# ScalarE pieces of their own and an earlier self-attention in the plan of a decoder layer

## The chip, the cores and the metric

The kernel runs on one core of a Trainium2 chip. It is one program that holds its data in SBUF and PSUM and gives work to TensorE (PE; matmuls and transposes), VectorE (DVE), ScalarE (ACT), GpSimd (POOL) and, for the DMA queues, SyncE (SP). The metric is the device time of one execution in microseconds. A time is a median of several runs; the profile is one execution of its own.

## What is computed

The reference is one decoder layer over x of 16 batches, 512 rows and 256 columns, in fp32. Cut to what matters:

```
# 1 self-attention without softmax, two key/value sets, 16 heads
q  = x + x Wq + bq;  k_i = x + x Wk_i + bk_i;  v_i = x + x Wv_i + bv_i      (i = 0, 1)
state = prod_i ( (k_i / 32)^T (v_i / 32) )            # per batch and head
x1 = layernorm( x + layernorm_gb(q state) Wo + bo )
# 2 cross-attention on 64 context rows per batch, 16 heads of 64
x2 = layernorm( x1 + softmax(q k^T / 8, masked) v Wout + b_out )
# 3 eight experts: softmax routing; each expert takes at most 1024 rows, in order
x3 = layernorm( x2 + sum_e w_e * relu(x2 W1_e) W2_e )    # rows past the capacity get no expert
```

With these inputs the capacity of 1024 rows is used up by the first two batches (the "head"), so the other 14 batches end with the last layer norm, and the loop over further batches at the end of the program runs zero times.

## The kernel before, in words

**Tiles.** A batch is four tiles of 128 rows. Self-attention (L614 to L726) never forms k and v: the stream of Gram matrices computes x^T x (ps_g, L555 and L560, and one transposed block ps_gt, L573) and key sums (ps_ks, L585); from them a batch takes ps_gk (L629), the two states (ps_s, L641), transposes of x (ps_t, L233), ps_m and ps_b from the state, then four pieces ps_o (L687), each followed on VectorE by an addition and the layer norm's statistics (L249, L250). `normalized` (L252 to L269) is the layer norm: on ScalarE a logarithm and an exponential of the variance (L261, L262), on VectorE the offset (`off`, L265), on ScalarE one Identity for each of four tiles (L267). Transposes of the result (ps_zt, L700), four pieces ps_p (L711), the second norm into x1 and the transposes to x1T follow; at the end POOL adds a bias to x1 (L725). Before the second norm a batch waits in the plan until routing of the batch two before is done, since x1 has two buffers. xt, z, zT and pT have one buffer each.

**Cross-attention** (L765 to L843). The keys are multiplied into the query weights once per two batches (kq, ps_kq, L751), the values into the output weights during set-up (ps_vo, L492): their product goes through four buffers `vst` (copies by ScalarE L186 or VectorE L188), is stored in 128 DMAs of 132 KB (L497) to vo_dram, and is fetched again as `vo` (L781, 512 DMAs, eight chunks a batch, of which six are fetched ahead). For each tile there are two halves: ps_sim (L814), on VectorE the maximum (L820) and the subtraction (L821), on ScalarE the exponential (L822). Then the softmax: sum and reciprocal on VectorE (L800, L801), the multiply on POOL (L802), and a transpose on VectorE into pT (L804). When all four tiles are in pT, ps_x follows (L834): 256 matmuls of 32 rows in a row, and an addition (L841).

**Routing** (L846 to L873) is a layer norm, for the head a transpose to head_T, and a softmax over eight experts in small VectorE operations (L858 to L865) with one exponential (L861). `ranks` (L875 to L920) gives each row its place in its expert, once. The **experts** (L929 to L976) are ps_h (L946), a Relu copy to hT on VectorE or ScalarE in turn (L954, L952), ps_e (L963) and a weighted addition (L970).

**The order of the work.** It is fixed when the program is built. Each stage is a Python generator in a `Stream`; `weave` (L1010 to L1027) takes one piece after the other, up to the next `yield`, from the ready stream with the smallest planned time `at + span * spent / total`. `spent` grows by `model.took`, TensorE's time for the piece as the planner's class `Model` (L28 to L102) reckons it. After `yield WAIT` a stream is ready only when its own work would be done, by the same reckoning; `until(...)` yields until a condition holds; `beside(st, gen)` adds a small stream that starts at the present time of `st`. `in_order` (L1029) then pins the instructions of PE, DVE, ACT and POOL in the order in which they were traced; each engine works in that order and stops at an instruction whose input is not ready. SP's DMAs are issued in their traced order too. With SETUP = 115 and STEP = 78, self-attention of batch b is planned at SETUP + (b − 1) · STEP (L1071), cross-attention at SETUP + b · STEP, routing at SETUP + (b + 1) · STEP, the experts from SETUP + 1.3 · STEP on.

Of the kernel before, what the change touches and what calls it, by code (L numbers as in the profile page):

```python
# [27 lines left out]
class Model:  # L28
# [2 lines left out]
    WIDE = {"PE": 0.25, "DVE": 0.15, "Activation": 0.15, "Pool": 0.15}  # L31

    def __init__(self, nc):
        self.nc, self.free, self.dma = nc, {}, 0.0
        self.made, self.used, self.slots, self.rows, self.seen = {}, {}, {}, P, 0

    def tile(self, name, key, bufs):
# [28 lines left out]
    def run(self):  # L66

        traced = self.nc.cur_bb.bb.instructions
        end = now = self.free.get("PE", 0.0)
        self.took = 0.0  # L70
        for ins in traced[self.seen:]:
            kind, engine = type(ins).__name__, str(ins.engine).split(".")[-1]
            aps = [[a.bass_ap for a in l if hasattr(a, "bass_ap")] for l in (ins.ins, ins.outs)]
            names = [[a.name for a in l] for l in aps]
            at = 0.0
            for made, used, l in ((1, 0, names[0]), (1, 1, names[1])):
                for n in l:
                    if kind == "InstDMACopy" and self.made.get(n, (0, 0))[1] == "SP":
                        continue
                    for known, book in ((made, self.made), (used, self.used)):  # L80
                        if known and n in book:
                            t, by = book[n]
                            at = max(at, t + (self.WIDE.get(by, 0.0) if by != engine else 0.0))
            if kind == "InstDMACopy":
                size = 4 * min(a.size() for l in aps for a in l)
                start = max(at, self.dma if now < 40 else 0.0)
                self.dma = start + size / 220e3
                done = self.dma + 2.0
            elif names[1]:
                start = max(at, self.free.get(engine, 0.0))  # L90
                done = self.free[engine] = start + self.duration(ins, kind, engine)
                if engine == "PE":
                    self.took += done - start
                else:
                    end = max(end, done + 0.15)
            else:
                continue
            for n in names[0] + names[1]:
                self.used[n] = max(self.used.get(n, (0.0, None)), (done, engine), key=lambda p: p[0])
            for n in names[1]:  # L100
                self.made[n] = (done, engine)
        self.seen, self.end = len(traced), end  # L102
        return end
# [13 lines left out]
def decoder_layer(  # L117
# [134 lines left out]
    def normalized(dst, src, NT=NT, mm=None):  # L252


        rstd = small.tile([P, NT], FP, tag="rstd", name="rstd")
        if mm is None:
            mm = moments(NT)
            for t in range(NT):
                moment(mm, t, src(t))
        mv = mm[1]  # L260
        nc.scalar.activation(rstd, mv[:, :, 1], AF.Ln, bias=eps)  # L261
        nc.scalar.activation(rstd, rstd, AF.Exp, scale=-0.5)  # L262
        yield WAIT
        off = small.tile([P, NT], FP, tag="off", name="off")
        nc.vector.scalar_tensor_tensor(off, mv[:, :, 0], -1.0, rstd, ALU.mult, ALU.mult)  # L265
        for t in range(NT):
            nc.scalar.activation(  # L267
                dst[:, t, :], src(t), AF.Identity, bias=off[:, t:t + 1], scale=rstd[:, t:t + 1]
            )  # L269


    with ExitStack() as att:
# [492 lines left out]
        def cross_attention(b, x1, x1T):  # L765


            bl = b % GB
            if bl == 0:
                yield from context_group(b // GB)  # L770
            kq = group[b // GB][:, :, bl].rearrange("p c r h j -> p c (r h j)")


            vos = []

            def load_vo():
                c = len(vos)
                t = wk2.tile([P, NH // 4, CX], FP, tag="vo", name="vo", bufs=6)
                h0 = c % 4 * NH // 4
                for q in range(P // 32):  # L780
                    nc.sync.dma_start(  # L781
                        out=t[q * 32:(q + 1) * 32], in_=vo_dram[b, c // 4 * 32:(c // 4 + 1) * 32, h0:h0 + NH // 4, :]
                    )
                vos.append(t)

            def load_first():
                yield from until(lambda: ("values", b // (B // 2)) in held)
                for _ in range(6):
                    load_vo()

            beside(cross_st, load_first())

            probsT = wk1.tile([P, 2 * NH, NT, 32], FP, tag="pT", name="pT")
            ready = []

            def softmax(t, s):
                sm = small.tile([P, NH], FP, tag="sm", name="sm")
                nc.vector.tensor_reduce(sm, s, AX.X, ALU.add)  # L800
                nc.vector.reciprocal(sm, sm)  # L801
                nc.gpsimd.tensor_mul(s, s, sm.unsqueeze(2).to_broadcast([P, NH, J]))  # L802
                yield WAIT
                nc.vector.transpose(probsT[:, :, t, :], s.rearrange("p h (a j) -> p (h a) j", a=2))  # L804
                ready.append(t)

            for t in range(NT):
                yield from until(lambda: len(ready) > t - 2)
                s = wk2.tile([P, NH, J], FP, tag="s", name="s")
                mx = small.tile([P, NH], FP, tag="mx", name="mx")  # L810
                for hf in range(2):
                    ps = bank("ps_sim")
                    for cc in range(NC):
                        nc.tensor.matmul(  # L814
                            ps, x1T[:, cc, t * P:(t + 1) * P], kq[:, cc, hf * 512:(hf + 1) * 512],
                            start=(cc == 0), stop=(cc == NC - 1),
                        )
                    hs = slice(hf * 8, (hf + 1) * 8)
                    sim = ps.rearrange("p (h j) -> p h j", j=J)
                    nc.vector.tensor_reduce(mx[:, hs], sim, AX.X, ALU.max)  # L820
                    nc.vector.tensor_sub(s[:, hs, :], sim, mx[:, hs].unsqueeze(2).to_broadcast([P, 8, J]))  # L821
                    nc.scalar.activation(s[:, hs, :], s[:, hs, :], AF.Exp, scale=SCALE)  # L822
                    yield
                beside(cross_st, softmax(t, s))
            yield from until(lambda: len(ready) == NT)
            yield from until(lambda: made(probsT))
            yield from until(lambda: len(vos) == 6 and made(*vos))
            ps = [bank("ps_x") for _ in range(NT)]
            for c in range(8):
                for i in range(NH // 4):  # L830
                    blk = (c % 4 * NH // 4 + i) * 2 + c // 4
                    for q in range(NT):
                        pq = slice(q * 32, (q + 1) * 32)
                        nc.tensor.matmul(  # L834
                            ps[q][:, :CX], probsT[pq, blk].rearrange("p t i -> p (t i)"), vos[c][pq, i, :],
                            start=(c == 0 and i == 0), stop=(c == 7 and i == NH // 4 - 1),
                        )
                if c < 2:
                    load_vo()
            for q in range(NT):  # L840
                nc.vector.tensor_add(x1[:, q, :], ps[q][:, :CX], x1[:, q, :])  # L841
            yield WAIT
# [167 lines left out]
        def weave():  # L1010
            model.run()
            while streams:
                clock = model.free["PE"] = model.free.get("PE", 0.0)
                now = [st for st in streams if st.ready <= clock]
                if not now:
                    model.free["PE"] = min(st.ready for st in streams)
                    continue
                st = min(now, key=Stream.time)
                wait = next(st.gen, "end")
                st.end = max(st.end, model.run())  # L1020
                st.spent += model.took
                if wait == "end":
                    streams.remove(st)
                elif wait == WAIT:
                    st.ready = st.end
                else:
                    st.ready = clock + (wait or 0.0)  # L1027
# [40 lines left out]

        def all_self_attention():
            for b in range(B):  # L1070
                self_st.plan(SETUP + (b - 1) * STEP, STEP, 16.5)  # L1071
                yield from until(lambda: b in grams and sums[b // QB][1] and "rb" in cs and made(grams[b], sums[b // QB][1][0]))
                yield from self_attention(b, done)

# [137 lines left out]
```

## Time and profile before

| | us |
|---|---|
| median of three runs | 1387.47 (1385.21 to 1389.51) |
| the profiled execution | 1389.4 |
| its span in the profile | 1387.6 |
| TensorE busy | 1365.9 |
| VectorE busy | 850.7 |
| ScalarE busy | 402.2 |
| GpSimd busy | 203.7 |

The mean clock granted to TensorE in the profiled execution was 0.994 of full speed. The chain of work that ended last runs for 89% of the span through TensorE, 5% through VectorE and 2% through DMA. By groups, the largest are ps_h (L946) with 239.1 us, ps_sim (L814) with 235.0 and ps_x (L834) with 234.9 us. DMA moved 153.57 MB, 111 GB/s in the mean.

How to read it: "busy" is the time that records of an engine cover; TensorE's records are pipelined, so a busy TensorE is not always one at its full pace. In a row of a group or a timeline, `out<-in` are the program's names of the tiles; in brackets is the idle time before an instruction and who ended it. A row of waits names the waiting instruction, the one that released it, the sum in us, the count and the longest. PEclk is the granted clock, in tenths in the slices and as a share in the tables by stage.

### The profile page before, as it was taken

What the parts mean: (1) busy time and instruction counts of PE and PEld (TensorE: products, weight loads), DVE (VectorE), ACT (ScalarE), POOL (GpSimd) and SP (SyncE); (2) the same over time, 40 slices, a digit from 0 to 9 for tenths busy, and PEclk for the clock granted to TensorE, in tenths of its full rate; (3) what the DMA queues carried; (4) which work ended last, traced back from release to release, by engine and by line L of the source; (5) the groups of instructions that cost most, each with busy time, mean ns of one, the idle gap of its engine ahead of it and who ended that gap; (6) DMA issues with size and microseconds to landing.
All of it is one profiled execution on the core that took longest, in us unless ns stands there. A gap on an engine that the chain in (4) does not pass through costs nothing.

```text
span 1387.6 us, 24209 instructions
## 1 busy us (share of the span) xinstructions
PE 1365.9 (98%) x9630; PEld 1077.9 (78%) x9630; DVE 850.7 (61%) x1957; ACT 402.2 (29%) x912; POOL 203.7 (15%) x140
## 2 busy tenths in 40 slices
PE   8999999999999999999999999999999999999997
PEld 5766576877878787878878787878888787878686
DVE  2445848466584848475584848475665939484744
ACT  1134224132232314142233323142323323232322
POOL 0001112112020111112020112112020202111200
PEclk9999999999999999999999999999999999999999
DMA  8657775511515153522606053513334061505211
GB/s 260 203 136 191 189 195 163 142 32 42 145 53 150 46 142 106 127 77 52 181 24 164 31 142 106 126 62 77 110 95 123 16 187 46 147 26 126 91 56 40
DMA packets 98372, 153.57 MB, mean 111 GB/s; under 512 B 15560, under 2 KB 70096, under 8 KB 98256
## 3 DMA queue, kind: packets, MB, share of 16 engines
q1 hardware_dynamic: 98256, 151.98, 40.1%
q8 instruction: 78, 1.28, 0.4%
q14 instruction: 38, 0.31, 0.1%
HBM read 114.71 MB, written 37.22 MB: 109 GB/s over the span
## 4 chain that ended last, share of the span: by engine, by line
PE 89%; DVE 5%; DMA 2%; SPq 1%; ACT 1%; issue 1%; ACTq 0%; DVEq 0%
PE ps_x L834 16%; PE ps_sim L814 15%; PE ps_e L963 15%; PE ps_h L946 15%; PE ps_gk L629 4%; PE ps_p L711 4%; PE ps_o L687 3%; PE ps_kv L437 3%; PE ps_t L233 2%; PE ps_kq L751 2%; PE ps_vo L492 2%; PE ps_s L641 2%; PE ps_g L555 2%; PE ps_zt L700 1%; PE ps_m L670 1%; PE ps_g L560 1%
## 5 line engine op out<-in xcount | busy, mean ns | idle before, releaser
L946 PE MATMUL ps_h<-head_T,wi 128*128 128x256 f32 x1024 | 239.1, 379 | 0.0
L834 PE MATMUL ps_x<-vo,pT 32*128 32x264 f32 x4096 | 234.9, 384 | 3.9 <-DVE pT L804 3.7
L814 PE MATMUL ps_sim<-kq,x1T 128*128 128x512 f32 x512 | 235.0, 593 | 0.0
L834 PEld LDWEIGHTS ps_x<-vo,pT 32*128 32x128 f32 x4096 | 211.5, 186 | 26.1 <-issue 5.6
L946 PEld LDWEIGHTS ps_h<-head_T,wi 128*128 128x128 f32 x1024 | 193.4, 190 | 38.8 <-issue 13.0
L802 POOL TENSOR_TENSOR s<-s,sm 128x1024 f32<-128x1024 f32 x64 | 121.7, 1901 | 539.8 <-DVE sm L801 501.4
L841 DVE TENSOR_TENSOR x<-ps_x,x 128x264 f32<-128x264 f32 x64 | 23.2, 426 | 226.3 <-PE ps_x L834 226.3
L822 ACT ACTIVATE s<-s 128x512 f32<-128x512 f32 x128 | 80.7, 630 | 276.1 <-DVE s L821 276.0
L814 PEld LDWEIGHTS ps_sim<-kq,x1T 128*128 128x128 f32 x512 | 94.5, 190 | 83.2 <-issue 74.5
L820 DVE TENSOR_REDUCE mx<-ps_sim 128x8 f32<-128x512 f32 x128 | 86.1, 673 | 42.0 <-PE ps_sim L814 41.6
L821 DVE TENSOR_TENSOR s<-ps_sim,mx 128x512 f32<-128x512 f32 x128 | 88.5, 692 | 4.4
L725 POOL TENSOR_TENSOR x<-x,bout 128x1056 f32<-128x1056 f32 x16 | 38.7, 2420 | 320.7 <-ACT hT L952 172.6
L804 DVE STREAM_TRANSPOSE pT<-s 128x1024 f32<-128x1024 f32 x64 | 78.6, 1228 | 7.0 <-POOL s L802 7.0
L952 ACT ACTIVATE hT<-ps_h 128x256 f32<-128x256 f32 x128 | 46.9, 376 | 119.9 <-PE ps_h L946 119.8
L701 ACT ACTIVATE zT<-ps_zt,shift,gain 128x512 f32<-128x512 f32 x32 | 23.2, 775 | 189.5 <-PE ps_zt L700 189.5
L800 DVE TENSOR_REDUCE sm<-s 128x16 f32<-128x1024 f32 x64 | 77.1, 1204 | 0.4 <-ACT s L822 0.4
L261 ACT ACTIVATE rstd<-bn_mv,eps 128x4 f32<-128x4 f32 (+1 forms) x70 | 20.7, 295 | 159.5 <-DVE bn_mv L250 156.0
L267 ACT ACTIVATE x<-x,off,rstd 128x264 f32<-128x264 f32 (+1 forms) x112 | 58.3, 591 | 29.3 <-DVE off L265 29.3
L687 PE MATMUL ps_o<-m,xT 128*128 128x264 f32 x256 | 66.7, 387 | 0.0
L954 DVE TENSOR_SCALAR hT<-ps_h 128x256 f32<-128x256 f32 x128 | 52.2, 409 | 22.5 <-PE ps_h L946 22.3
L711 PE MATMUL ps_p<-wo,zT 128*128 128x264 f32 x256 | 63.1, 387 | 0.0
L629 PE MATMUL ps_gk<-wk,g 128*128 128x256 f32 x256 | 61.2, 382 | 0.0
(174 smaller groups left out, 1897.4 us busy)
## 6 DMA issues: line engine op xcount, KB each, us to landing
vo<-vo_dram SPq DMA_DIRECT2D x512, 132.0 KB, 4.2
vo_dram<-vst SPq DMA_DIRECT2D x128, 132.0 KB, 2.4
xt<-in_x_dram SPq DMA_DIRECT2D x16, 512.0 KB, 4.0
wi<-L_ffn_experts_inter_dram SPq DMA_DIRECT2D x8, 1024.0 KB, 5.3
gx<-in_x_dram SPq DMA_DIRECT2D x15, 512.0 KB, 4.2
x_rest<-x SPq DMA_DIRECT2D x14, 512.0 KB, 3.1
out_dram<-x SPq DMA_DIRECT2D x14, 512.0 KB, 2.9
kT<-k_dram SPq DMA_DIRECT2D x8, 512.0 KB, 3.3
```

What stands on the lines that cost most here:

```text
L629: nc.tensor.matmul(ps[:, :C], blk, wk[:, j, k, :], start=(j == 0), stop=(j == NC - 1))
L687: nc.tensor.matmul(ps[:, :CX], xT[:, cc, t * P:(t + 1) * P], m[:, cc, :], start=(cc == 0), stop=(cc == NC - 1))
L711: nc.tensor.matmul(ps[:, :CX], zT[:, cc, t * P:(t + 1) * P], wo[:, cc, :], start=(cc == 0), stop=(cc == NC - 1))
L802: nc.gpsimd.tensor_mul(s, s, sm.unsqueeze(2).to_broadcast([P, NH, J]))
L804: nc.vector.transpose(probsT[:, :, t, :], s.rearrange("p h (a j) -> p (h a) j", a=2))
L814: nc.tensor.matmul(ps, x1T[:, cc, t * P:(t + 1) * P], kq[:, cc, hf * 512:(hf + 1) * 512], start=(cc == 0), stop=(cc == NC - 1),)
L820: nc.vector.tensor_reduce(mx[:, hs], sim, AX.X, ALU.max)
L821: nc.vector.tensor_sub(s[:, hs, :], sim, mx[:, hs].unsqueeze(2).to_broadcast([P, 8, J]))
L822: nc.scalar.activation(s[:, hs, :], s[:, hs, :], AF.Exp, scale=SCALE)
L834: nc.tensor.matmul(ps[q][:, :CX], probsT[pq, blk].rearrange("p t i -> p (t i)"), vos[c][pq, i, :], start=(c == 0 and i == 0), stop=(c == 7 ...
L946: nc.tensor.matmul(ps[:, :TB], wi[:, cc, f * P:(f + 1) * P], head_T[b][:, cc, t0 * P:t0 * P + TB], start=(cc == 0), stop=(cc == NC - 1),)
L963: nc.tensor.matmul(ps[:, :C], hT[f][:, t * P:(t + 1) * P], wo_[:, f, :], start=(f == 0), stop=(f == NF - 1),)
```

## The change

There are three edits, and the number of instructions on each engine stays the same.

1. `normalized` gets a `yield WAIT` ahead of the logarithm and one ahead of the four Identities, so that both ScalarE steps are pieces of their own.
2. In cross-attention the exponential of each half becomes a small stream of its own, put beside; the softmax of a tile waits in the plan until both of its halves are done. Since the planner now runs more than once within a piece, `took` is set to zero in `weave`.
3. Self-attention of batch b is planned at SETUP + (b − 1.6) · STEP in place of (b − 1).

```diff
@@ Model.run
         traced = self.nc.cur_bb.bb.instructions
         end = now = self.free.get("PE", 0.0)
-        self.took = 0.0
@@ normalized
         mv = mm[1]
+        yield WAIT
         nc.scalar.activation(rstd, mv[:, :, 1], AF.Ln, bias=eps)
         nc.scalar.activation(rstd, rstd, AF.Exp, scale=-0.5)
         yield WAIT
         off = small.tile([P, NT], FP, tag="off", name="off")
         nc.vector.scalar_tensor_tensor(off, mv[:, :, 0], -1.0, rstd, ALU.mult, ALU.mult)
+        yield WAIT
         for t in range(NT):
@@ cross_attention
-            def softmax(t, s):
+            def exponentials(s, hf, halves):
+                hs = slice(hf * 8, (hf + 1) * 8)
+                nc.scalar.activation(s[:, hs, :], s[:, hs, :], AF.Exp, scale=SCALE)
+                halves.append(hf)
+                yield
+
+            def softmax(t, s, halves):
+                yield from until(lambda: len(halves) == 2 and made(s))
                 sm = small.tile([P, NH], FP, tag="sm", name="sm")
...
+                halves = []
                 mx = small.tile([P, NH], FP, tag="mx", name="mx")
...
-                    nc.scalar.activation(s[:, hs, :], s[:, hs, :], AF.Exp, scale=SCALE)
+                    model.run()
+                    beside(cross_st, exponentials(s, hf, halves))
                     yield
-                beside(cross_st, softmax(t, s))
+                beside(cross_st, softmax(t, s, halves))
@@ weave
                 st = min(now, key=Stream.time)
+                model.took = 0.0
                 wait = next(st.gen, "end")
@@ all_self_attention
-                self_st.plan(SETUP + (b - 1) * STEP, STEP, 16.5)
+                self_st.plan(SETUP + (b - 1.6) * STEP, STEP, 16.5)
```

More of the change, by code (lines that the diff above doesn't have):

```diff
@@ L33, in __init__ @@
     def __init__(self, nc):
-        self.nc, self.free, self.dma = nc, {}, 0.0
+        self.nc, self.free, self.dma, self.took = nc, {}, 0.0, 0.0
         self.made, self.used, self.slots, self.rows, self.seen = {}, {}, {}, P, 0
```

## The prediction

> **What bounds the kernel now.** I read the page's busy shares and slices first, then TensorE's waits, then a table by stage, and last the timelines of the queues behind the waits that the table left.
>
> ```profile
> PE 1365.9 (98%) x9630; PEld 1077.9 (78%) x9630; DVE 850.7 (61%) x1957; ACT 402.2 (29%) x912; POOL 203.7 (15%) x140
> ...
> PE   8999999999999999999999999999999999999997
> ```
>
> TensorE is the bound, and no other engine is near. The change removes no matmul: both built programs have 5060 matmuls, 1957 VectorE, 912 ScalarE and 789 DMA instructions. Only order and waits can pay. How much is there to win? I took each matmul kind's pitch from stretches without a wait (the 256-column one 0.432 us: two records of 0.216; 512 columns 0.858; 264 columns 0.445; a batch's 256 ps_x records 14.15) and multiplied by the counts: 1334.8 us. With 3.1 us before the first matmul and 6.7 after the last one's start, 1387.6 − 1344.6 = 43 us are excess. By place: 7.7 in 0–50 us, 4.0 in 50–100, 12.9 in 100–200, 3.1 in 200–300, 5.1 in 300–350, then 0.05 to 0.6 for each 50 us, and 3.9 after 1250. So a change of order can win something between 50 and 340 us, and little else.
>
> ```profile
> PE ps_x L834 <- DVE pT L804: 3.7, 2, 3.2
> ...
> PE ps_e L963 <- DVE hT L954: 1.8, 1, 1.8
> PE ps_vo L492 <- DVE u L570: 0.8, 1, 0.8
> PE ps_vo L492 <- ACT st L186: 0.7, 1, 0.7
> ```
>
> The next table has microseconds, busy time of PE, PEld, DVE, ACT, POOL, then granted clock, DMA share and GB/s.
>
> ```profile
> 66.70:73.50 6.80, 6.80 (x26) 5.96 (x26) 2.18 (x3) 0.00 (x0) 0.00 (x0) 0.50 0.00 0
> 107.00:143.00 36.00, 35.38 (x213) 23.80 (x212) 19.59 (x50) 16.49 (x41) 4.99 (x4) 1.00 0.81 200
> 143.00:188.00 45.00, 43.33 (x196) 25.90 (x194) 36.14 (x71) 17.14 (x41) 10.09 (x7) 1.00 0.64 174
> ...
> 336.30:339.80 3.50, 2.98 (x28) 2.66 (x32) 0.37 (x1) 0.00 (x0) 1.54 (x1) 0.51 0.02 5
> 340.00:400.00 60.00, 60.00 (x445) 47.88 (x438) 36.82 (x84) 15.95 (x35) 6.22 (x3) 1.00 0.47 134
> ```
>
> Row one: TensorE looks busy, yet at half clock; it costs 6.80 × 0.50 = 3.4 us. Row four: half clock again, 3.5 × 0.49 = 1.7. The last row is the steady state: nothing to win. Two queues make the rest. SP's stores of the values:
>
> ```profile
> 80.42 36.82 SPq L497 DMA_DIRECT2D vo_dram<-vst  x56
> ...
> 177.73 17.20 SPq L497 DMA_DIRECT2D vo_dram<-vst  x24
> 195.02 17.29 SPq L781 DMA_DIRECT2D vo<-vo_dram  x32
> ```
>
> And VectorE ahead of batch 2's ps_x:
>
> ```profile
> 333.50 1.90 POOL L802 TENSOR_TENSOR s<-s,sm 128x1024 f32<-128x1024 f32 x1 [8.42 <-DVE ks L590]
> ...
> 333.76 1.68 DVE L865 TENSOR_TENSOR w_all<-w_all,rm 128x32 f32<-128x32 f32 x1
> 335.43 1.25 DVE L804 STREAM_TRANSPOSE pT<-s 128x1024 f32<-128x1024 f32 x1
> 336.82 5.47 PE L834 MATMUL ps_x<-vo,pT 32*128 32x264 f32 x68 [3.25 <-DVE pT L804]
> ```
>
> 56 stores in 36.82 us are 0.66 us each, 1.3 per tile of values; vst has four buffers, and its copies sat 31.1 us in 42 waits for these stores. TensorE's excess at L492 adds up to 9.1 us, in seven places.
>
> **What is won.** (1) At 66.7 us the half clock follows a stretch of 8-column matmuls and transposes (L404, L528, L537) in a row. In the changed order ps_m, ps_b, eight ps_o and a ps_g lie between them, and no narrow stretch is longer than 2.8 us. The Trainium skill ("TensorE: Matmul & The Clock Gate", section "HAM oscillation — how this bites in real kernels") asks only that TensorE be not idle for more than some 3.4 us. By that rule this place was never at risk and mending it wins nothing; the row, 0.50 with PE busy throughout, says it was: −3.4, less 0.4 because ps_m and ps_b now follow close behind the states, −3.0. (2) Self-attention 1 and 2 now give TensorE other work among the values. At 0.64 us a store, SP's demand outran TensorE's work by up to 6.6 us before (32.6 against 26.0 us of work at 142–182); in the new order by at most 3.2 (and by 2.4 once earlier). Four buffers of 1.3 us absorb the first part. I scale 9.1 to 2.8: −6.3. (3) Batch 0's ps_x at 201 us waits 1.4 us for vo chunks issued behind the 24 stores above; in the new order eight stores and one load are ahead of them: −1.4. (4) The waits between 204 and 255 (ps_gt 0.4, transposes 0.9, ps_x of batch 1 0.7): −2.0. (5) Batch 2's ps_x: 3.4 waited and 1.7 at half clock: −5.1. (6) At the end ps_tot's wait of 0.4–0.5 is gone: −0.5. The ps_e wait of 1.8 (hT queued behind the ranks' 8.3 us on VectorE) stays. Sum: −18.3.
>
> **What is paid.** (7) ps_zt of batch 2. TensorE has 2.6 us of Gram work left when VectorE still owes: hop 0.2, max 0.67, subtraction 0.69, four statistics 4 × 0.535 = 2.1, offset 0.15; then four ScalarE identities, 2.07: 5.9 − 2.6 = +3.2. (8) x1T of batch 2 now stands directly ahead of batch 1's ps_x. VectorE's queue up to the softmax's reciprocal: hop 0.2, max 0.72, subtraction 0.69, transpose 1.2, hT 0.41, sum 1.24, reciprocal 0.25: 4.7. Then come POOL's multiply, and on VectorE routing's small ones with L865 and the offset, and the identities (2.1). Here a rule speaks against the change. The Trainium skill ("SBUF — State Buffer", section "SBUF: two separate sides") says that VectorE with two SBUF inputs and a GpSimd operation that reads SBUF lock each other out for a whole instruction. The trace agrees: L865's median is 0.19 us, and the one above took 1.68 and ended with POOL's L802. With that lock: 4.7 + 1.9 to POOL's end + 0.3 for L865 and the offset + 2.1 + 0.6 for three hand-overs = 9.6 against 7 us of TensorE work: 2.6 late. Without it pT's own chain (4.7 + 1.9 + 1.25 and hops, 8.1 against 7.5) leaves 0.65. I take +2.6, since the order puts them side by side as it did at 333 us. (9) The same pattern one batch on (x1T of batch 3, ps_x of batch 2): nearest row, the 3.25 at 336.8: +3.2. (10) Each of the three bubbles is about as long as the one that was followed by half clock; at one in four for each and 1.7 us: +1.3. Sum: +10.3.
>
> **What costs nothing.** The exponentials and norm steps as pieces of their own stand later in ScalarE's order. ScalarE is 29% busy; behind a waiting exponential (0.63 us) stand hT copies of 0.38, which ps_e needs some 3 us later. Its cover is the time from a batch's last ps_sim to its first ps_x: in the new order 9.9 to 19.6 us of other matmuls from batch 3 on (9.3 to 13.5 before), against 8.2 for max, subtraction, exponential, sum, POOL multiply, transpose and hops, and 12.1 with POOL's 2.42 of L725 ahead of it. The added "until" in the softmax is a wait of the plan and puts no instruction into a queue. Moved DMAs: the earlier xt load has SP's queue before it, and landing takes 4.0 us where ps_t is more than 10 off; wi and wo_ land in 5.3 with 9.9 between issue and use.
>
> So −18.3 + 10.3 = −8.0: 1389.4 → 1381.4 for the profiled execution. That stands 1.9 above the median; on the median, 1387.5 − 8.0 = 1379.5.
>
> **Rivals.** A, the bubbles of (7) to (9) are covered, because VectorE's statistics come a little earlier than I queue them: −18.3 + 2 to 5: 1371 to 1374. For it: only tenths decide. Against: all three chains are serial. B, no difference: the stores go on setting the pace, since 128 × 0.64 = 82 us of SP have to fit in before batch 0's ps_x either way (so −3 instead of −6.3), and the three bubbles all draw half clock (+3.8 more): −0.9, 1386.5. Also possible in this form: the pieces move nothing that TensorE waited for. C, slower: the chain of (8) recurs. With self-attention 0.6 batch further on, x1T stands directly ahead of ps_x in about eight batches; where the work between is less than about 12 us, the identities behind a locked VectorE come late, and TensorE stops in order. Eight times 2.6 is +20.8, with −8.0 in all +12.8: 1400. For it: batch 15 has 9.9 and batch 5 11.7 us. Against: the others have 12.6 or more, and 9.3 in the order before stopped only once.
>
> **How the numbers follow.** Chances: my sum (1374–1383) 0.52, A 0.10, B 0.22, C 0.16. Three runs of before differ by 0.3%, about what a measurement can tell from no change: 4.2 us, so faster is below 1383.3 and slower above 1391.6. Of B, a little lies below; of C, a little within: faster 0.65, same 0.20, slower 0.15. The range goes from A's lower end to just past no change, 1371 to 1392; what is left out is most of C and a tail below.
>
> **What would show it.** Right: no half clock near 66–74 us; waits at L492 down by some 6 us; the wait of ps_x for pT near 337 replaced by waits of ps_zt for zT's input z (L267) and of ps_t for x1 (L267) between 200 and 340; from 350 us TensorE full. Wrong: half clock in the first 100 us as before or at several new bubbles (B), or repeated waits of ps_t or ps_x, of 2 to 3 us, with a clock below 1.0 after batch 3 (C).

## The result, and the profile after

The changed kernel takes 1390.66 us (median of 12 runs, 1387.21 to 1396.55), the kernel before in the same series 1386.62 (1382.08 to 1391.17). The ratio is 1.0034, with a 95% interval of 1.002 to 1.0048: some 4 us slower. The prediction said 8 us faster. The time lies inside the stated range of 1371 to 1392, near its upper end. By the prediction's own bounds of 4.2 us either way that is "the same", to which it gave 0.20; the interval of the ratio puts it on the slower side.

The profiled execution took 1390.38 us with a span of 1388.7. First its page, with busy time by engine:

```profile
PE 1362.8 (98%) x9630; PEld 1074.4 (77%) x9630; DVE 826.6 (60%) x1957; ACT 403.7 (29%) x912; POOL 203.8 (15%) x140
```

Then its TensorE's waits (sum in us, count, longest):

```profile
PE ps_t L232 <- ACT x L268: 4.6, 11, 2.1
PE ps_zt L701 <- ACT z L268: 3.1, 4, 2.6
...
PE ps_vo L493 <- ACT vst L185: 1.8, 1, 1.8
PE ps_e L973 <- DVE hT L964: 1.4, 1, 1.4
```

TensorE is still the bound, with the same matmuls. The 3.7 us that ps_x waited for pT are gone, as is ps_tot's wait. In their place TensorE waits for z and for x, both written by the Identities of a layer norm (L268 here; the changed file has other line numbers than the one before). The table by stage (us, busy time of PE, PEld, DVE, ACT, POOL, granted clock, DMA share, GB/s) answers to the one of before:

```profile
66.70:73.50 6.80, 6.80 (x46) 6.21 (x46) 5.37 (x16) 1.09 (x3) 1.85 (x2) 1.00 0.00 0
229.90:233.30 3.40, 3.40 (x9) 1.85 (x8) 1.91 (x3) 3.30 (x6) 3.40 (x5) 0.50 1.03 384
257.20:260.60 3.40, 3.23 (x22) 2.50 (x25) 0.81 (x1) 0.76 (x2) 1.70 (x1) 0.50 0.52 147
345.00:400.00 55.00, 55.00 (x442) 44.51 (x435) 31.23 (x77) 12.06 (x28) 5.78 (x3) 1.00 0.51 146
```

The half clock near 67 us is gone, but two new windows of half clock stand right after two of the new bubbles (waits of TensorE). The last row shows that the steady state has nothing to lose or win.

**A second trace of before.** The profiled execution that the prediction rests on took 1389.4 us, 2.8 above the median of 12. So I ran the same kernel again for its trace.

> The kernel before, unchanged, a second look. Theory H (the profiled execution of before happened to draw more half-clock windows than usual: three of 3.41 us in 66.7-73.5 and 336.3-339.7, each 1.7 us lost, on top of the start): this look shows none or one window at 66.7 us, and a span near 1384.5 to 1386. Rival S (the half clock at 66.7 and 336 is a fixed part of this order): the same three windows and a span of 1387 to 1388.

It took 1385.85 us, with a span of 1384.1. Its table by stage:

```profile
66.70:73.50 6.80, 6.80 (x49) 6.09 (x49) 3.37 (x5) 0.72 (x2) 0.00 (x0) 1.00 0.00 0
332.90:336.30 3.40, 3.34 (x32) 2.99 (x36) 0.00 (x0) 0.00 (x0) 1.09 (x1) 0.50 0.02 5
```

In the same stretch, with the same order, TensorE got 49 records through at full clock where the first trace had 26 at half. That half clock is a matter of one execution and no fixed part of the order: 3.4 us that the first trace showed and this one did not. So theory H holds for 67 us, with a span 0.4 us below what it said. The window at 333 us, after the wait of 3.2 for pT, is in both traces, as rival S had it; but it is no fixed part of the order either: a later run of the same order (before_merge) waits the same 3.2 us there and has no window behind it. From here on this second trace, close to the median, stands for before.

With the prediction's own measure (TensorE's excess: its time less what its matmuls take at their pitches) the two kernels compare by place like this, in us:

| place | before, second trace | after | moved | the prediction's terms |
|---|---|---|---|---|
| 0–50 | 8.2 | 7.6 | −0.6 | 0 |
| 50–100 | 1.0 | 2.4 | +1.4 | (1) −3.0 |
| 100–200 | 11.7 | 7.7 | −4.0 | (2), (3) −7.7 |
| 200–350 | 8.5 | 16.3 | +7.8 | (4), (5), (7) to (10) +3.2 |
| 350–1250 | 6.2 | 8.3 | +2.1 | 0 |
| 1250 to the end | 3.9 | 2.6 | −1.3 | (6) −0.5 |
| sum | 39.4 | 44.8 | +5.4 | −8.0 |

The two spans differ by 4.6 us, the medians by 4.0; the places add up to 5.4, so the measure is good to some 0.8 us. Four places make most of the miss: 50–100, 100–200, 200–350 and 350–1250.

### The profile page after: what moved, and what is told of

It is laid out like the page before. It is cut to its first block, busy times and chain, and to the rows that moved or that the text cites. A ratio compares the mean times of both kernels' runs of the same rounds, so it can differ in the third digit from the quotient of the medians.

```text
span 1388.7 us, 24177 instructions
## 1 busy us (share of the span) xinstructions
PE 1362.8 (98%) x9630; PEld 1074.4 (77%) x9630; DVE 826.6 (60%) x1957; ACT 403.7 (29%) x912; POOL 203.8 (15%) x140
## 4 chain that ended last, share of the span: by engine, by line
PE 92%; DVE 4%; DMA 2%; ACT 1%; SPq 0%; issue 0%; ACTq 0%; DVEq 0%
PE ps_x L844 17%; PE ps_sim L823 15%; PE ps_h L956 15%; PE ps_e L973 15%; PE ps_o L688 4%; PE ps_gk L630 4%; PE ps_kv L438 4%; PE ps_p L712 3%; PE ps_t L232 3%; PE ps_kq L752 2%; PE ps_s L642 2%; PE ps_vo L493 2%; PE ps_g L556 2%; PE ps_m L671 1%; PE ps_zt L701 1%; PE ps_g L561 1%
## 5 line engine op out<-in xcount | busy, mean ns | idle before, releaser
L823 PE MATMUL ps_sim<-kq,x1T 128*128 128x512 f32 x512 | 240.4, 596 | 0.3 <-DVE vst L187 0.3
L844 PEld LDWEIGHTS ps_x<-vo,pT 32*128 32x128 f32 x4096 | 208.5, 186 | 22.0 <-issue 2.2
L268 ACT ACTIVATE x<-x,off,rstd 128x264 f32<-128x264 f32 (+1 forms) x112 | 58.4, 593 | 28.4 <-DVE off L265 28.3
L438 PE MATMUL ps_kv<-cT,wT 128*128 128x512 f32 x128 | 59.0, 597 | 0.9 <-DVE vst L187 0.9
L712 PEld LDWEIGHTS ps_p<-wo,zT 128*128 128x128 f32 x256 | 48.6, 190 | 12.2 <-issue 3.8
L185 ACT COPY xT<-ps_t 128x512 f32<-128x512 f32 x16 | 9.4, 587 | 166.4 <-PE ps_t L232 166.4
```

What stands on the lines that cost most here:

```text
L438: nc.tensor.matmul(ps, wT[:, cc, r % 4 * P:(r % 4 + 1) * P], cT[:, cc, q * 512:(q + 1) * 512], start=(cc == 0), stop=(cc == NC - 1),)
L712: nc.tensor.matmul(ps[:, :CX], zT[:, cc, t * P:(t + 1) * P], wo[:, cc, :], start=(cc == 0), stop=(cc == NC - 1))
L823: nc.tensor.matmul(ps, x1T[:, cc, t * P:(t + 1) * P], kq[:, cc, hf * 512:(hf + 1) * 512], start=(cc == 0), stop=(cc == NC - 1),)
L844: nc.tensor.matmul(ps[q][:, :CX], probsT[pq, blk].rearrange("p t i -> p (t i)"), vos[c][pq, i, :], start=(c == 0 and i == 0), stop=(c == 7 ...
```

## Experiments

All ratios are to the kernel before, run in the same series; brackets hold the 95% interval. Differences in us are the ratio less one, times 1386.6 us. "Window" means a stretch of 3.41 us at half clock, which costs 1.7 us of TensorE's work.

**The parts alone.** First the shift without the pieces:

```diff
-                self_st.plan(SETUP + (b - 1) * STEP, STEP, 16.5)
+                self_st.plan(SETUP + (b - 1.6) * STEP, STEP, 16.5)
```

> The kernel before with the shift alone: self-attention planned at b - 1.6 in place of b - 1, ScalarE steps inside their pieces as before. Theory P (the shift makes the change: it puts x1T of batches 2 and 3 straight ahead of ps_x and ps_zt behind a thin cover, and gives the values other work): most of the change's effect, +2 to +6 us against before, with waits of ps_zt or ps_t of 2 to 5 us between 200 and 350. Rival E (the pieces make it: exponentials and norm steps later in ScalarE's order): within 1.5 us of before.

Measured 1.0055 (1.004 to 1.0071), +7.6 us. The longest new wait, beside smaller ones for z and pT:

```profile
PE ps_h L946 <- ACT hT L952: 3.1, 1, 3.1
```

It ends at 256.6 us. The time is a little above what theory P said, and the stall is at the expected place but not of the expected kind: not x or z, but an hT copy. The trace shows what held the copy up (in this file L860 is routing's subtraction, L861 its exponential):

```profile
253.63 1.90 POOL L802 TENSOR_TENSOR s<-s,sm 128x1024 f32<-128x1024 f32 x1 [9.28 <-DVE w_all L858]
253.76 1.82 DVE L860 TENSOR_TENSOR w_all<-w_all,rm 128x32 f32<-128x32 f32 x1
255.62 0.23 ACT L861 ACTIVATE w_all<-w_all 128x32 f32<-128x32 f32 x1 [4.03 <-DVE w_all L860]
...
256.11 0.94 ACT L952 ACTIVATE hT<-ps_h 128x256 f32<-128x256 f32 x3
```

Routing's subtraction took 1.82 us beside POOL's multiply in place of 0.19, and ScalarE's hT copies stood behind routing's exponential.

Next the pieces without the shift:

```diff
-                self_st.plan(SETUP + (b - 1.6) * STEP, STEP, 16.5)
+                self_st.plan(SETUP + (b - 1) * STEP, STEP, 16.5)
```

> The changed kernel with the plan of self-attention back at b - 1: the ScalarE pieces alone. Theory P: within 2 us of before, and the waits for x and z (L268) between 200 and 350 us gone. Rival E: +2 to +6 us, with ScalarE's pieces behind the waits of TensorE.

Measured 1.0158 (1.013 to 1.0185), +21.9 us: more than either theory said. TensorE's waits:

```profile
PE ps_t L232 <- ACT x L268: 3.7, 3, 3.3
...
PE ps_vo L493 <- ACT vst L185: 3.0, 4, 1.7
PE ps_gt L574 <- DVE g L187: 2.4, 1, 2.4
...
PE ps_x L844 <- DMA vo<-vo_dram: 1.1, 1, 1.1
```

Between 100 and 250 us it loses 31.4 us where before loses 14.6, and five windows between 209.8 and 233.7 go with these waits. Some 8 us more than in before are lost between 350 and 1250 us, among them two waits of ps_m for the state and two of ps_x for pT, of about 1 us each or less.

Then the exponentials alone:

```diff
         mv = mm[1]
-        yield WAIT
         nc.scalar.activation(rstd, mv[:, :, 1], AF.Ln, bias=eps)
...
-        yield WAIT
         for t in range(NT):
```

> As pieces_only, but only the exponentials are pieces of their own; the two new waits inside the layer norm are taken out. Theory P: within 2 us of before and of pieces_only. Rival E, if the norm's waits are what costs: 2 to 5 us below pieces_only.

Measured 1.0039 (1.0024 to 1.0054), +5.4 us. Its table by stage:

```profile
247.00:253.00 6.00, 3.66 (x18) 2.89 (x17) 5.47 (x13) 1.63 (x6) 4.26 (x4) 1.00 0.33 87
253.20:260.00 6.80, 5.99 (x56) 4.87 (x60) 0.76 (x1) 1.24 (x3) 0.00 (x0) 0.50 0.14 42
333.00:338.00 5.00, 3.01 (x14) 2.30 (x13) 4.79 (x14) 2.79 (x7) 2.06 (x3) 1.00 0.00 0
338.50:345.00 6.50, 5.83 (x52) 5.83 (x56) 0.62 (x1) 0.00 (x0) 1.79 (x1) 0.50 0.13 36
```

Batches 1 and 2 both stop at ps_x for 3.3 to 3.5 us, waiting for pT, with two windows behind each. Batch 2's stop is that of before; batch 1's is new:

```profile
246.87 1.90 POOL L808 TENSOR_TENSOR s<-s,sm 128x1024 f32<-128x1024 f32 x1 [5.23 <-DVE sm L807]
247.58 1.24 DVE L866 TENSOR_TENSOR w_all<-x_head,rb 128x32 f32<-128x32 f32 x1
...
248.92 2.34 POOL L704 TENSOR_TENSOR xt<-xt,bo 128x1024 f32<-128x1024 f32 x1
249.08 2.23 DVE L868 TENSOR_TENSOR w_all<-w_all,rm 128x32 f32<-128x32 f32 x1
...
252.72 1.24 DVE L810 STREAM_TRANSPOSE pT<-s 128x1024 f32<-128x1024 f32 x1
```

Two small operations of routing (L866 and L868 in this file) ran beside POOL's and took 3.5 us together, ahead of the last transpose into pT; in the second trace of before the same two took 0.24 and 0.19. So what the exponential as a piece of its own cost here is a new order that put routing's operations beside POOL's, more than time on ScalarE; "costs nothing" was wrong all the same. Theory P's "within 2 us" missed for both kernels without the shift, while E's own difference, 2 to 5 us for the norm's waits, was too small: they account for 16.5. Shift (+7.6) and pieces (+21.9) do not add up to the change (+4): each plan is a new order, and its losses are its own.

Last the shift with the exponentials, without the norm's waits (the exps_only edit on the changed kernel):

> The changed kernel without the two new waits in the layer norm: exponentials as pieces and the shift to b - 1.6 stay. If the norm's pieces are what makes the shifted order bearable or bad cannot be told from the runs so far (with the plan at b - 1 they took exponentials alone from +0.4% to +1.6%). Theory G (the loss comes from x1 held back by routing and from the values' stores, whatever pieces ScalarE has): within 3 us of the changed kernel, 1388 to 1394, with a wait of ps_t or ps_x of 2 us or more near 250 and near 340. Rival E (the norm's pieces cost): 4 us or more below the changed kernel.

Measured 1.0045 (1.003 to 1.006), +6.2 us, within 3 us of the changed kernel, as G said. But the waits near 257 and 340 us are only 1.2 and 1.9 us in TensorE's excess, less than the 2 expected, and the wait of ps_zt near 226 is gone (no wait of ps_zt for z is longer than 0.3); 2.6 are lost at 407 instead, and 1.2 to 1.9 at three later places. In the total, under the shift, the norm's waits are neither the cure nor the cost; they decide where the stops stand.

**The stores of the values.** One DMA of 128 partitions takes the place of two of 64. It leaves the order on the four compute engines as it was, instruction for instruction.

```diff
-                    for bl in range(GB):
-                        nc.sync.dma_start(
-                            out=vo_dram[(q * NG + g) * GB + bl, :, r * 2:(r + 1) * 2, :],
-                            in_=vst[bl * J:(bl + 1) * J],
-                        )
+                    b0 = (q * NG + g) * GB
+                    nc.sync.dma_start(
+                        out=vo_dram[b0:b0 + GB, :, r * 2:(r + 1) * 2, :].rearrange("b j h c -> (b j) h c"),
+                        in_=vst,
+                    )
```

> The changed kernel with each values tile stored by one DMA of 128 partitions in place of two of 64 (64 stores in place of 128); the order on TensorE, VectorE, ScalarE and GpSimd is the same, instruction for instruction. Theory V (SP's pace of 0.64 us a store still holds TensorE at ps_vo: 6.5 us of excess there in the changed kernel): the copies' waits for stores fall to a third or less, and the time falls by 4 to 6 us, to 1385 to 1387 on the scale of the changed kernel's 1390.7. Rival W (the copies wait for the stores' landing, which a larger store does not shorten, or TensorE would wait for something else): within 1.5 us.

> The kernel before with one store per values tile, same order otherwise. Theory V: its 9 us of excess at ps_vo go to 2 or less and ps_x of batch 0 no longer waits for its last chunks: 6 to 9 us below before, 1377 to 1380. Rival W: within 1.5 us of before.

On the changed kernel: 1.0001 (0.9989 to 1.0013), 4.6 us below the change's 1.0034. On before: 0.9953 (0.9933 to 0.9973), −6.5 us. Both lie where theory V had them. The rows of the tile vst (duration min/median/max in ns; idle time in us, times), first the copies' waits in before, then the changed kernel's rows:

```profile
  DMA vo_dram<-vst: 31.1, 42
```

```profile
L498 SPq DMA_DIRECT2D vo_dram<-vst x128: 445/587/1920, 87.6 to 224.2; - x128
...
  DMA vo_dram<-vst: 31.3, 36
```

With one store a tile:

```profile
L498 SPq DMA_DIRECT2D vo_dram<-vst x64: 319/372/1654, 86.0 to 215.8; - x64
...
  DMA vo_dram<-vst: 7.7, 9
```

The change left the copies' waits for stores as they were: 31.1 us before, 31.3 after. It only moved some to where TensorE does not stop for them. With half the stores a quarter remains, and TensorE's excess in 100–200 us falls from 7.7 to 4.4 in the changed kernel and from 11.7 to 7.2 in the one before.

What remains near 92 us with one store a tile is one stop of 2.4 us. Its timeline, from the changed kernel with both repairs (below), whose stop at the same place is 2.5, and the landing of its four stores:

```profile
88.34 2.10 ACT L268 ACTIVATE x<-xt,off,rstd 128x264 f32<-128x264 f32 x4
...
90.35 1.19 ACT L185 COPY vst<-ps_vo 128x264 f32<-128x264 f32 x4
90.51 0.38 SPq L612 DMA_DIRECT2D xt<-in_x_dram  x1
...
91.00 2.37 SPq L498 DMA_DIRECT2D vo_dram<-vst  x4
...
95.91 0.38 ACT L185 COPY vst<-ps_vo 128x264 f32<-128x264 f32 x1 [3.14 <-DMA vo_dram<-vst]
```

```profile
DMA to landing us min/median/max: 4.8/5.1/5.4
```

The four Identities of an x1 stand ahead of the copies on ScalarE, and the 512 KB load of the next xt stands ahead of their stores on SP; the four stores behind it landed in 4.8 to 5.4 us, where the median of all stores of that run is 3.0. Both come from self-attention placed among the values. This is read from the timeline; no run moved the Identities or the load away.

**Routing's place in the plan.** Routing's stream has a total of 1.0, and the head's eight transposes count for 0.88 of it, so after them its planned time leaps 0.88 × 78 = 69 us; its softmax (L868 to L875 in the changed file) comes late for batches 0 and 1. A total of 100 removes the leap.

```diff
-                routing_st.plan(SETUP + (b + 1) * STEP, STEP, 1.0)
+                routing_st.plan(SETUP + (b + 1) * STEP, STEP, 100.0)
```

> The changed kernel with one number of the plan changed: routing's stream is planned with a total of 100 in place of 1, so that its head transposes no longer put it 69 us further on in the plan, and its softmax follows at once. Theory G (in the changed kernel x1 of batches 2 and 3 comes late because it waits in the plan for the routing of batches 0 and 1, whose softmax the plan held back; so both stand straight ahead of ps_x): the waits of ps_t for x at 256 and 342 us shrink from 3.7 and 2.5 us to below 1 each and the half-clock window near 257 goes; the wait of ps_zt near 226 stays; the time falls by 5 to 8 us. Rival C (x1T ahead of ps_x is late by its own chain on VectorE and ScalarE, whatever routing does): within 2 us of the changed kernel, with the same waits a few us to one side.

> The kernel before with the same one number changed. Theory G: the softmax of batch 1's routing no longer stands in VectorE's queue ahead of the last pT of batch 2 (333.8 us, locked 1.7 us behind GpSimd), so ps_x of batch 2 waits less than 1.5 in place of 3.3 us, without half clock after it: 3 to 5 us below before. Rival C: the wait of ps_x for pT stays at 3 us or more; within 1.5 us of before.

On the changed kernel: 0.996 (0.9944 to 0.9975), against 1.0034 without it: some 10 us. On before: 0.9951 (0.993 to 0.9971), −6.8 us. The waits of the changed kernel with it:

```profile
PE ps_zt L701 <- ACT z L268: 3.1, 1, 3.1
...
PE ps_t L232 <- ACT x L268: 0.5, 3, 0.2
```

The waits for x went from 4.6 us to 0.5, and the excess in 250–350 us from 9.1 to 1.1. The wait of ps_zt stayed, as expected. In before, ps_x's wait of 3.2 for pT is gone from the list of waits altogether. Both gains exceed what theory G said (5 to 8, 3 to 5) by a little. Rival C, that x1T is late by its own chain wherever it stands, falls: the chain is the same, it comes earlier, and nothing waits for it:

```profile
241.86 0.19 DVE L870 TENSOR_TENSOR w_all<-w_all,rm 128x32 f32<-128x32 f32 x1
...
247.66 0.29 ACT L261 ACTIVATE rstd<-bn_mv,eps 128x4 f32<-128x4 f32 x1
...
252.83 2.09 ACT L268 ACTIVATE x<-xt,off,rstd 128x264 f32<-128x264 f32 x4
...
255.81 1.04 PE L232 MATMUL ps_t<-ident,x 128*128 128x128 f32 x8
```

How the bubble came about shows in the changed kernel's timeline without the repair:

```profile
252.19 1.90 POOL L810 TENSOR_TENSOR s<-s,sm 128x1024 f32<-128x1024 f32 x1 [3.99 <-DVE w_all L868]
252.32 1.82 DVE L870 TENSOR_TENSOR w_all<-w_all,rm 128x32 f32<-128x32 f32 x1
254.17 0.23 ACT L871 ACTIVATE w_all<-w_all 128x32 f32<-128x32 f32 x1 [3.46 <-DVE w_all L870]
...
254.45 0.30 ACT L261 ACTIVATE rstd<-bn_mv,eps 128x4 f32<-128x4 f32 x1
...
255.28 2.10 ACT L268 ACTIVATE x<-xt,off,rstd 128x264 f32<-128x264 f32 x4 [0.29 <-DVE off L265]
255.94 0.33 PE L232 MATMUL ps_t<-ident,x 128*128 128x128 f32 x1 [2.08 <-ACT x L268]
```

The statistics of this x were complete at 244 us (L249, 243.77 and 0.18). Its logarithm ran at 254.45: the plan holds x1 of batch 2 back until routing of batch 0 is done. Then routing's subtraction L870, not its last multiply as I had it (L875 here, L865 in before), met POOL's multiply and took 1.82 us in place of 0.19, and routing's exponential, the logarithm, the offset and the Identities all queued behind it.

**Both repairs together.**

> The changed kernel with both repairs, one store per values tile and routing's total of 100. If the two causes are separate, the ratios multiply: 1.0001 x 0.996 / 1.0034 = 0.993 of before, 1376 to 1380. If both took away the same wait, no better than after_route alone, 0.996.

> The kernel before with both repairs. Separate causes: 0.9953 x 0.9951 = 0.990 of before, 1372 to 1375, and the fastest version so far; then the change itself would still cost some 0.3% on top of both repairs. If the same: 0.995.

> The ScalarE pieces alone (plan at b - 1) with both repairs. pieces_only lost most at ps_x of batch 0 (7.3 us, after a wait for vo, at half clock), at ps_vo (some 8 us) and at ps_t waiting for x near 226 us (3.3). Theory V and G: with half the stores the chunks land in time, so ps_x of batch 0 and ps_vo lose less than 4 us together, and the time falls from +22 us to within 5 us of before. Rival E (ScalarE's pieces themselves come late): still 10 us or more above before.

The changed kernel with both: 0.9936 (0.9922 to 0.995), 1378.07 us. Before with both: 0.9908 (0.9892 to 0.9924), 1374.89 us, the fastest kernel of the study, 12.8 us below before. Both as expected for separate causes. The change still costs 0.9936 / 0.9908, 0.28%, or 3.2 us between the medians (the intervals overlap a little, so its size is uncertain). In the traces the difference is at the wait of ps_zt (5.6 against 2.1 us of excess in 200–250), at the stop near 92 us (3.6 against 1.0 in 50–100) and at one x1T near 1023 (1.1); the changed order is better in 100–200 (4.4 against 6.6).

The pieces alone with both repairs: 1.003 (1.0021 to 1.004), +4.2 us where they were at +21.9. Against before that is what theories V and G said. But before gains from the repairs too: against before with both (1374.89) the pieces alone (1390.89) still cost 16.0 us, so most of their price is their own, and the change's small total means that pieces and shift together cost far less than the pieces alone. Two of the stops:

```profile
PE ps_t L232 <- ACT x L268: 3.4, 1, 3.4
...
PE ps_x L844 <- DMA vo<-vo_dram: 2.2, 1, 2.2
```

The first is the 3.3 of pieces_only, which neither repair touches: with its steps apart, x1's offset stands on VectorE behind the four statistics of another layer norm, that of x_head (208.81 to 210.94 us), and its Identities on ScalarE behind that norm's logarithm. The second is part of 7.1 us that ps_x of batch 0 still loses:

```profile
186.50 0.38 SPq L990 DMA_DIRECT2D wi<-L_ffn_experts_inter_dram  x1
186.94 0.46 SPq L995 DMA_DIRECT2D wo__1959<-n_L_ffn_experts_out_dram  x1
187.45 21.68 SPq L782 DMA_DIRECT2D vo<-vo_dram  x31
```

Two loads of experts' weights, 1 MB each, stand directly ahead of the chunks that ps_x needs, and the chunks then land in up to 9.2 us (median 4.5). ps_x waited 2.2 us for a chunk and ran through two windows. Whether moving these loads would mend it was not tried.

## Why the prediction was wrong

The direction failed because the gains were counted too high, (1) to (3) by 6.7 us in all, and the stops that the new order makes too low, by 4.6 us with their half clock; the ScalarE pieces, put at nothing, were not free.

- **What bounds, and where time could be won:** right. TensorE at 98%, and the whole study moved time only where it was said to be, mostly between 50 and 340 us: two edits there won 12.8 us with TensorE's work unchanged.
- **Step (1), −3.0:** wrong, by half on the mean and by all of it against the trace that stands for before. It treated the half clock at 67 us as a part of the order; it is one that this order draws in some executions. Eight traced executions have the same TensorE order up to there (before twice, before with each repair and with both, the pieces alone with and without repairs, the exponentials alone). Four show it, three with two windows and one with one: (3 × 3.4 + 1.7) / 8 = 1.5 us on the mean, not 3.4. None of the four with the changed order shows it, so the direction may hold; but the changed order lost 1.4 more in 50–100 us, mostly at a stop of 1.1 near 92 us for the values' copies. The Trainium skill ("TensorE: Matmul & The Clock Gate", section "HAM oscillation — how this bites in real kernels") asks for no idle gap above some 3.4 us. By that rule no window would have come at 67 us, where TensorE was never idle by the records, nor behind the new bubbles of 2.6 and 2.1 us. The measurement decides: all three came (the one at 67 us in half the traces), and what draws them stays open.
- **Steps (2) and (3), −7.7:** the mechanism was right (one store in place of two takes away just this), the size was not: −4.0 in 100–200 us. The surplus of SP's demand over TensorE's work was scaled down to 2.8 us of excess, but the pieces of self-attention that were to give cover brought their own: four Identities (2.1 us) ahead of the copies on ScalarE and a 512 KB load ahead of the stores. "Moved DMAs cost nothing" failed here: the cover was reckoned for xt's own reader, not for the stores queued behind the load.
- **Steps (4) and (5), −7.1:** right. None of these waits is left at its place; (5)'s 3.2 us and one window were in both traces of before.
- **Step (7), +3.2:** right, a little small (its own terms come to 3.3, not 3.2): 2.6 us of waiting and about 1.3 more while the transposes went at the Identities' pace, 0.50 us each.
- **Step (8), +2.6:** right in place, too small: 2.2 of waiting and 1.2 at the Identities' pace, 3.4 before its half clock. The lock fell on the subtraction, so routing's exponential and the norm's logarithm came after it as well. The sum had the last multiply locked, side by side with POOL, because the row of before had it so. What stood behind it, that x1 was held back by routing's gate, was in the code and not in the sum.
- **Step (9), +3.2:** right in size: 2.3 at x1T, where the last multiply was locked beside POOL (1.64 us at 339.7) as the prediction had it, and 0.7 at ps_gt shortly before.
- **Step (10), +1.3:** too small. The two traces with the changed order between 200 and 345 us (the changed kernel, and the one with merged stores) have two and three windows there, 3.4 and 5.1 us.
- **ScalarE's pieces at nothing:** in the changed order right from 350 us on but for two x1T waits of 0.6 and 1.1 us (+2.1 in all there), wrong for the first batches, as exps_only and pieces_only show, and in the old order (pieces_only) wrong from 350 us on as well. It weighed the softmax's own chain and ScalarE's load; the pieces also changed what stands beside and ahead of what on VectorE and GpSimd. The cover (9.9 to 19.6 us) was counted from batch 3 on only.
- **Rival C** foretold the right side by a mechanism that does not exist in that form: the chain recurs in each batch and is covered from batch 4 on but for those two waits. **Rival B** came nearest in its reasons (less from the stores, half clock at new bubbles).

By size, the miss of 13.4 us in the table is 4.4 in 50–100 us (3.0 of it is (1)), 3.7 at (2) and (3), 4.6 at the bubbles and their windows, and 2.1 in later batches, less 1.4 at the start and end. The averages over all runs say the same. If a run's lost time at a clock c is 1388 × (1 − c), the changed kernel loses 7.3 us to the clock and before, in three series, 5.1 to 6.0; the rest of the 4.0 us, some 2 to 3, is waiting.

## What to carry to other kernels

One profiled execution shows what one execution did: before a term is put on a half-clock stretch, compare that execution's time with the median of the runs, and count only what other traces of the same order show too. When work is moved under a stall to cover it, count what that work puts into each queue, ScalarE's and SP's too, ahead of the instructions that stall. When a part of a change is judged on top of a repair, compare it with the old kernel that has the same repair: here that turned +4.2 us into +16.0. When a moved piece comes to stand at a bad place, look for the gate that put it there: a plan's total of 1 in place of 100 held routing back by 69 us of planned time and cost more than the whole change.

## What the hardware showed beside that

- A store of 128 partitions took SP less time to issue (0.37 us median) than one of 64 partitions with half the bytes (0.58 us); I had expected a gain from the number of stores alone.
- With one order of instructions the same stretch of 8-column matmuls and transposes ran at full clock in some executions and at half in others, with TensorE busy throughout in both. Most of the spread between the runs of one kernel goes with the mean granted clock: the changed kernel's 12 runs have mean clocks from 0.991 to 0.997 and spans from 1394.9 to 1385.5, and 0.006 of the span is 8.3 us of those 9.4.
- After the same wait of 3.2 us for pT, with the same order on the compute engines, half clock followed in both traces of before and not in before_merge.
- Routing's additions, subtractions and multiplies of 128x32 on VectorE, where they stood beside a GpSimd operation on other tiles, lasted until it ended: 1.24 to 2.23 us, against a median of 0.18 to 0.19. Several of the stops between 245 and 345 us, in four of the orders tried, have one of them in their chain.
